# A GPS graph layer on one core: the last two node tiles go through one block per expert, the first returned rows go into places of sent tokens, the input flag is spread over the edge loop, chunks get smaller

## The chip, the core and the metric

The kernel runs on one core of one Trainium2 chip. The core has five engines with an instruction stream each: TensorE (PE, matrix products and transposes), VectorE (DVE), ScalarE (ACT), GpSimd (POOL) and SyncE (SP, which here only issues transfers). They share the on-chip memories SBUF (128 partitions) and PSUM (where matmuls write, in banks) and are kept in step by semaphores. Transfers to and from DRAM run on 16 DMA engines. A transfer is issued by an instruction on some engine's queue; an indirect one (rows picked by an index list) is issued by POOL here.

The metric is the device time of one execution, in microseconds (us). The kernel before takes 1828.77 us, the median of 8 runs between 1819.89 and 1846.31.

## The reference

All data are fp32. There are 6250 nodes with 256 features, and 106,250 edges, sorted by their destination, with 64 attributes each. The layer adds a message-passing branch and a linear-attention branch to the nodes, and then a feed-forward step in which each node uses one of 32 experts:

```python
xn = _layernorm(x)
# message passing: gather, project, silu, sum by destination, normalize
msgs = jnp.concatenate([xn[src], edge_attr], axis=-1)
msgs = jax.nn.silu(msgs @ W + b)
gnn  = _layernorm(jax.ops.segment_sum(msgs, dst, 6250), eps=1e-3) * gamma + beta
# linear attention, 8 heads of 64, k and v normalized over a head
dots = einsum('bhnd,bhne->bhde', k, v)
mix  = einsum('bhnd,bhde->bhne', q, dots) / n  @ Wout.T + bout
x = x + gnn + mix
# feed-forward with one expert per node
xf  = _layernorm(x)
idx = argmax(xf @ router_w.T + router_b)          # of 32
h   = relu(xf @ W1[idx] + b1[idx])                # 256 -> 64
out = x + relu(h @ W2[idx] + b2[idx])             # 64 -> 256
```

Since the projection is linear, the node part of `msgs @ W` is computed once per node and gathered afterwards.

## The kernel before

**Tiles.** The nodes are 49 tiles of 128 rows (the last has 106). `X` holds all of them in SBUF, `wide` holds their normalized, transposed rows and, once these are no longer needed, expert weights and tokens. The edges are 208 groups of 512; two groups make a step of the sum by destination.

**First stage** (`stage_one`, L254 to L484). Per pair of tiles: load, layernorm, transpose (L353), project (L363), add the bias (L369), store `proj` to DRAM. `columns` (L372) turns the source indices (at pair 3) and the destinations' offsets (at pair 10) into the layout of the loop, the latter after POOL has made them (at pair 6). At the end, `row_of` is made and then a flag: whether the destinations fit the windows that the loop assumes. This is a chain on DVE (L460 to L480), a matmul with ones (L482, `pflag`) and a copy into `unlike`. The flag is read only at the very end of the program, where a general path would follow if it were set. The pool `early` and the PSUM pool `pre_ps` are closed when `stage_one` returns; the loop's PSUM pool and the attention's SBUF pool open afterwards.

**Edge loop** (L1562 to L1603). For each group: four indirect gathers of `proj` rows on POOL, three groups ahead (L1432); the edge attributes turned (L1448, copied by ACT, L1452); their product `h` (L1571); DVE adds the gathered rows (L1573); ACT applies silu (L1589). Every second group, `level1` (L1526) and `level2` (L1553) sum the messages by destination. A tile whose edges are all in is closed, and a chunk of tiles (`CHUNKS`) is finished when its last tile is closed.

**The planner** (`Work`, L1287). All other work stands beside the loop as pieces: Python generators that write some instructions and then yield an estimated cost for PE and DVE, and a delay in turns. In each of the loop's turns `step` lets pieces advance until an allowance (2.7 us of PE, 3.8 us of DVE) is spent. In the last `QUIET = 4` turns only urgent pieces advance. After the loop `drain` (L1349) writes out what is left by a model of when the engines are free. So the order of instructions on every engine is fixed when the program is built. The pieces are: the attention's weights and batches, node chunks, rounds, clears of the blocks (L688), loads of the experts' weights.

**Chunks** (`Nodes.chunk`, L731). Finished tiles get the sum's layernorm (`sums_end`), the attention's product (`mixing`, L720), a second layernorm, the router's logits in groups of two tiles (transposes L784, `lg` L772), the argmax as a row of 0 and 1 (`hot`, L820), each token's rank within its expert (`prank`, L839 and L842; `ahead`, L846), and its place in a block (`slot`, L965). Then `send` (L1051) scatters each tile's rows into `xs` in DRAM.

**Rounds** (`Nodes.round`, L1265; `ROUNDS`). A round holds the tokens of some tiles as blocks of 64. The first round takes tiles 0 to 27 with 76 blocks, each with an expert chosen at run time; the next four (tiles 28 to 33, 33 to 38, 38 to 42, 42 to 47) have one block per expert. Four blocks make a quad (`tokens`, `layers`): load `xb` (L1066, on SP's queue), transpose (`pt`, L1088), first layer (`phid`, L1100; relu by ACT, L1110), second layer (`py`, biases L1124 and product L1135), relu (L1144), store to `ys` (L1146). When all quads of a round are done, `collect` (L1232) fetches the rows back by tile with indirect gathers (`fetch`, L1225), DVE adds them to `X` (L1248), and SP stores two tiles to the output (L160). In the drain the fetches' destinations are a ring of 4 `ot` pairs and 3 pairs of `wide`.

**The last round** is `(2, 0)`: tiles 47 and 48 are not sent. `dense` (L875 to L948) runs all 32 experts, two at a time, over their 234 rows: turned rows (L891) and turned `hot` rows (L895), bias of the second layer (L906), and for each of 16 pairs the first layer (L922), a masking product that pushes all rows of other experts below zero (L931), relu (L940), and the second layer (L914), summed over all experts in PSUM. Then relu, add and store.

**PSUM tags.** `kv` (two buffers) is shared by the attention's products, `lg`, `prank`, `phid` and, in the loop, both `py`; `t` (two buffers) by all transposes and `po`; `sum` and `h` by the loop's sums and products, and in the drain by `py`.

Of the kernel before, what the change touches and what calls it, by code (L numbers as in the profile page):

```python
# [31 lines left out]
CHUNKS = (6, 6, 6, 5, 5, 5, 5, 4, 3, 2, 2)  # L32
CH = max(CHUNKS)
FIRST = (2, 4, 6, 10, 13, 14)
AB = 2
# [6 lines left out]
BESIDE = 2  # L42
AHEAD_US = 1.0
# [4 lines left out]

ROUNDS = ((28, 76), (5, None), (5, None), (4, None), (5, None), (2, 0))
QUIET = 4  # L50
FAR = 3e38
# [11 lines left out]
def kernel(  # L63
# [190 lines left out]
    def stage_one(early, pre_ps):  # L254
# [133 lines left out]
        for j in range(NP + 1):  # L388
# [4 lines left out]
            if j == 3:  # L393
                nc.gpsimd.tensor_copy(src_f, src_r)
                columns(lambda b: src_f[:, b, :], src_T)
            if j == 6:
                nc.gpsimd.tensor_copy(dst_f, dst_r)
                nc.gpsimd.tensor_sub(rel, dst_f, dst_f[:, :, 0:1].to_broadcast([P, EB, P]))
            if j == 10:
                columns(lambda b: rel[:, b, :], rel_T)  # L400
# [56 lines left out]

# [5 lines left out]
        low, high = bounds(g_f, [P, EB], "tb")  # L463
        bad = early.tile([P, EB], F32, name="bad")
        nc.vector.tensor_reduce(bad, rel, axis=AX.X, op=ALU.max)
        nc.vector.tensor_scalar(bad, bad, float(SPAN), None, op0=ALU.is_ge)
        for source, op, limit, test in (
# [3 lines left out]
        ):  # L471
            some = early.tile([P, EB], F32, name="some", bufs=2)
# [8 lines left out]
        pb = bank("o", [1, 1], "pflag", 3)  # L481
# [134 lines left out]
    class Nodes:  # L616


        def __init__(self, pool, rounds, in_order):
# [36 lines left out]
            self.ring, self.returns = 7 if in_order else 4, 0  # L656
            self.started = self.through = self.flying = self.held = 0
            self.idle = pool.tile([1, 1], F32, name="idle")
            self.dense_in = False
# [43 lines left out]
        def sums_end(self, t0, t1):  # L703
# [3 lines left out]
            yield 0.0, 1.9, 1  # L707
            for t in range(t0, t1):
# [4 lines left out]
                if t % 3 == 2 or t == t1 - 1:  # L713
                    yield 0.0, 1.3, 1
# [16 lines left out]
        def chunk(self, t0, t1):  # L731
# [11 lines left out]
            for t in range(t0, t1):  # L743
# [6 lines left out]
                yield pe, dve + 0.6, int(t == t1 - 1)  # L750
            self.at[t0] = 1
            while not behind(2):
                yield 0.0, 0.0, 1
# [7 lines left out]
            yield 0.0, 1.9, 1  # L761
            logit = self.pool.tile([P, CH, NE], F32, name="logit", bufs=2)
            pairs = [list(range(t, min(t + 2, t1))) for t in range(t0, t1, 2)]
            turned = {}
            for i in range(len(pairs) + 2):
                pe = dve = 0.0
                if i >= 2:
                    lg = self.bank("kv", [P, 2, NE], "lg")
# [10 lines left out]
                    pe, dve = pe + 0.5, dve + 0.3  # L779
                if 1 <= i <= len(pairs):  # L780
                    for t in pairs[i - 1]:
# [3 lines left out]
                        turned[t] = self.pool.tile([P, DC, P], F32, name="xfT", bufs=2)  # L785
                        nc.scalar.copy(turned[t], pt)
                    pe += 0.5
# [36 lines left out]
            if r.dense:  # L824
                yield 0.0, 1.9, 1
                self.work.add(self.dense(t0, t1), rank=2)
                while not behind(4):
                    yield 0.0, 0.0, 1
                nc.vector.tensor_add(flag, self.over, unlike)
                return  # L830
# [26 lines left out]
            if r.own:  # L857
# [6 lines left out]
                if t1 == r.t1:  # L864
                    most = small.tile([1, 1], F32, name="most")
                    nc.vector.tensor_reduce(most, self.so_far[0:1, 0, :], axis=AX.X, op=ALU.max)
                    self.count(most, HB)
                self.at[t0] = 4
# [5 lines left out]

        def dense(self, t0, t1):  # L875


            m, pool = t1 - t0, self.last
            n = (m - 1) * P + rows_of(t1 - 1)
            of = [slice(k * P, min((k + 1) * P, n)) for k in range(m)]  # L880
            w = [q.stop - q.start for q in of]
            ident_b = pool.tile([P, P], BF16, name="ident_b")
            nc.vector.tensor_copy(ident_b, ident)
            far = pool.tile([NE, NE], BF16, name="far")
            nc.vector.tensor_scalar_mul(far, ident[:NE, :NE], -FAR)
            xT = pool.tile([P, DC, n], F32, name="xT")
            for k in range(m):
                pt = self.bank("t", [P, DC, P], "pt")
                feats = wide[:, t0 + k, :].rearrange("p (q c) -> p c q", c=DC)
                for c in range(DC):  # L890
                    nc.tensor.transpose(pt[:, c, :], feats[:, c, :], ident)  # L891
                nc.scalar.copy(xT[:, :, of[k]], pt[:, :, : w[k]])
            ph = self.bank("kv", [NE, n], "phot")
            for k in range(m):
                nc.tensor.matmul(  # L895
                    ph[:, of[k]], self.hot[:, t0 + k, :], ident_b[:, : w[k]], start=True, stop=True
                )
            hotT = pool.tile([NE, n], F32, name="hotT")
            nc.vector.tensor_copy(hotT, ph)
            other = pool.tile([NE, n], BF16, name="other")  # L900
            nc.vector.tensor_scalar(other, ph, -1.0, 1.0, op0=ALU.mult, op1=ALU.add)
            yield 1.0, 0.6, 1
            self.dense_in = True
            py = [self.bank("sum", [P, D], f"py{k}") for k in range(m)]
            for k in range(m):
                nc.tensor.matmul(py[k][: w[k], :], hotT[:, of[k]], self.b2_sb[:NE, :], start=True, stop=False)  # L906
            yield 0.9, 0.0, 0
            hids, pairs = {}, NE // BB
            for q in range(pairs + 2):
                if q >= 2:  # L910
                    hid = hids.pop(q - 2)
                    w2_q = wide[:, (q - 2) // 2 * QB + BB + q % 2, :]
                    for k in range(m):
                        nc.tensor.matmul(  # L914
                            py[k][: w[k], :], hid[:, of[k]], w2_q, start=False, stop=(q - 2 == pairs - 1)
                        )
# [905 lines left out]
```

## Time and profile before

| | us |
|---|---|
| median of 8 runs | 1828.77 (1819.89 to 1846.31) |
| the profiled execution | 1844.18, of it 1842.5 in the span |
| first stage, to the last projection's end | 79 |
| edge loop, to the last sum (L1553) | about 99 to 1699.3 |
| from there to the end | 143.2 |

| engine | busy us | share of the span | instructions |
|---|---|---|---|
| PE | 1281.7 | 70% | 8301 |
| DVE | 825.4 | 45% | 2107 |
| ACT | 567.2 | 31% | 1046 |
| POOL | 940.6 | 51% | 1046 |

The DMA engines moved 227.6 MB, 124 GB/s on average. Mean granted clock of PE: 0.81 of full speed. The profile is of one execution, which is 15.4 us above the median of the plain runs.

How to read the lines further on. A group line gives the source line, the engine, the operation, output and inputs by the program's names, shapes and count; after the bar its busy time in us and the mean of one in ns; after the second bar the engine's idle time just before those instructions and what ended most of it ("issue" means nothing that the profile shows). A line of waits gives engine and line, what it waited for, the total in us, how often, and the longest. A timeline line gives start, duration, engine, line, operation, and in brackets the idle time before it with what ended it. A line of windows is explained where it is used.

### The profile page before, as it was taken

Reading aid. Unit: us, or ns where it says so; the run is one execution under the profiler, and the core shown is the slowest. Engines: PE = TensorE matmul, PEld = TensorE weight load, DVE = VectorE, ACT = ScalarE, POOL = GpSimd, SP = SyncE. Lnnn points to the kernel's source line nnn. Section 1 sums busy time; section 2 is a strip of 40 time slices with the busy share of each in tenths; the row PEclk is TensorE's granted clock in tenths of the full one; section 3 lists DMA queues with packets and bytes.
Section 4 is the critical chain, followed back from the end, with each engine's and each line's share of the span. In section 5 each row is a group of like instructions: output and inputs, shape, how many; then the busy total and the mean of one; then the engine's idle time right before and its main releaser. Section 6 shows DMA issues by size and latency. Waiting matters only on the chain. (4 is left out here: it accounts for less than half of the span.)

```text
span 1842.5 us, 24393 instructions
## 1 busy us (share of the span) xinstructions
PE 1281.7 (70%) x8301; PEld 740.5 (40%) x8301; DVE 825.4 (45%) x2107; ACT 567.2 (31%) x1046; POOL 940.6 (51%) x1046
## 2 busy tenths in 40 slices
PE   6747888788858888677766652655776667676557
PEld 5624444444434444444434421333443334343324
DVE  7734555555545565465554532332333133434420
ACT  4524444344334344222322211222222123232213
POOL 4535665666646566655654666453343434441541
PEclk9968989998979989877877766776777678877669
DMA  6383333343323334633432343455454444342443
GB/s 218 128 268 97 111 110 102 104 111 105 106 80 106 89 106 120 207 90 85 109 97 78 105 145 118 136 159 148 128 149 125 121 134 131 115 118 68 123 161 128
DMA packets 243794, 227.60 MB, mean 124 GB/s; under 512 B 130920, under 2 KB 213836, under 8 KB 243660
## 3 DMA queue, kind: packets, MB, share of 16 engines
q0 software_dynamic: 44384, 121.18, 22.3%
q1 hardware_dynamic: 91096, 77.41, 13.1%
q10 hardware_dynamic: 108180, 27.34, 6.5%
q8 instruction: 69, 1.13, 0.3%
q14 instruction: 65, 0.53, 0.1%
HBM read 180.14 MB, written 45.70 MB: 123 GB/s over the span
## 5 line engine op out<-in xcount | busy, mean ns | idle before, releaser
L1432 POOL DMA_INDIRECT gat<-proj,src_T x831 | 800.8, 964 | 744.1 <-issue 598.3
L1573 DVE TENSOR_TENSOR gat<-h,gat 128x1024 f32<-128x1024 f32 x208 | 254.2, 1222 | 452.8 <-PE h L1571 134.1
L1571 PE MATMUL h<-ge,eT 64*128 64x256 f32 x1664 | 284.2, 449 | 140.6 <-DVE gat L1573 59.5
L1571 PEld LDWEIGHTS h<-ge,eT 64*128 64x128 f32 x1664 | 170.2, 210 | 252.2 <-issue 154.7
L1589 ACT ACTIVATE gat<-gat 128x1024 f32<-128x1024 f32 x208 | 219.9, 1057 | 167.9 <-DVE gat L1573 116.2
L1553 PE MATMUL sum<-part,s 128*128 128x256 f32 x400 | 138.1, 475 | 94.8 <-DVE s L1542 71.8
L540 PE MATMUL kv<-kv_w,wide 128*128 128x512 f32 x392 | 197.9, 650 | 3.2 <-DVE kv_w L518 3.2
L1452 ACT COPY eT<-pt 128x256 f32<-128x256 f32 x208 | 77.5, 373 | 348.2 <-remote 179.1
L1526 PE MATMUL po<-gat,s 128*32 128x256 f32 x1664 | 147.7, 453 | 11.7 <-issue 10.7
L1535 ACT COPY part<-po 128x256 f32<-128x256 f32 x104 | 38.7, 372 | 377.0 <-PE po L1526 181.4
L1553 PEld LDWEIGHTS sum<-part,s 128*128 128x128 f32 x400 | 86.0, 234 | 133.1 <-DVE s L1542 79.5
L540 PEld LDWEIGHTS kv<-kv_w,wide 128*128 128x128 f32 x392 | 79.5, 215 | 85.6 <-issue 80.5
L1448 PE MATMUL pt<-ident,ea 128*128 128x128 f32 x416 | 99.7, 325 | 9.8 <-DVE dots L575 4.1
L1094 DVE COPY xbT<-pt 128x512 f32<-128x512 f32 x39 | 26.9, 689 | 160.7 <-remote 76.1
L1526 PEld LDWEIGHTS po<-gat,s 128*32 128x32 f32 x1664 | 52.4, 124 | 91.5 <-issue 75.6
L1448 PEld LDWEIGHTS pt<-ident,ea 128*128 128x128 f32 x416 | 45.0, 152 | 89.8 <-issue 68.1
L547 DVE TENSOR_REDUCE var<-sq 128x16 f32<-128x1024 f32 x49 | 59.7, 1218 | 46.0 <-ACT sq L546 26.7
L1124 PE MATMUL py<-b_sb,choseno 32*64 32x256 f32 x152 | 29.5, 491 | 66.2 <-ACT hid L1110 19.8
L720 PE MATMUL pres<-mix,wide 128*128 128x256 f32 x196 | 60.5, 446 | 20.5 <-DVE experto L1030 8.8
L1051 POOL DMA_INDIRECT xso<-wide,slot x47 | 47.2, 1005 | 51.4 <-DVE slot L965 27.1
L543 ACT COPY kv<-kv 128x512 f32<-128x512 f32 x98 | 54.5, 578 | 34.5 <-PE kv L540 19.0
L1124 PE MATMUL py<-b_sb,ident 32*64 32x256 f32 x256 | 36.2, 465 | 41.5 <-ACT hid L1110 19.4
(298 smaller groups left out, 1533.1 us busy)
## 6 DMA issues: line engine op xcount, KB each, us to landing
ea<-in_edge_attr_dram ACTq DMA_DIRECT2D x203, 128.0 KB
gat<-proj,src_T POOLq DMA_INDIRECT x831
xso<-zero SPq DMA_DIRECT2D x51, 256.0 KB
xb<-xso SPq DMA_DIRECT2D x51, 256.0 KB
yso<-xb SPq DMA_DIRECT2D x51, 256.0 KB
proj<-pr SPq DMA_DIRECT2D x24, 256.0 KB
out_dram<-X SPq DMA_DIRECT2D x22, 256.0 KB
w1t<-in_L_ffn_W_dram SPq DMA_DIRECT2D x76, 64.0 KB
```

What stands on the lines that cost most here:

```text
L540: nc.tensor.matmul(b, xnT(t0 + j, c), kv_w[:, c, s * F : (s + 1) * F], start=(c == 0), stop=(c == DC - 1))
L547: nc.vector.tensor_reduce(var[:, j * 2 * HEADS : (j + 1) * 2 * HEADS], sq, axis=AX.X, op=ALU.add)
L720: nc.tensor.matmul(p, xnT(t, c), mix[:, c, :], start=(c == 0), stop=(c == DC - 1))
L1124: nc.tensor.matmul(py[j][i * HB : (i + 1) * HB, :], one_of(b, rows).to_broadcast([NE, HB]), self.b2_sb[rows, :], start=True, stop=False, t ...
L1432: nc.gpsimd.indirect_dma_start(out=gat[:n, k % 2, k // 2, :], out_offset=None, in_=proj[:], in_offset=bass.IndirectOffsetOnAxis(ap=src_T[: ...
L1448: nc.tensor.transpose(pt[:, j, :], ea[:, 2 * j : 2 * j + 2, :].rearrange("p k d -> p (k d)"), ident)
L1452: nc.scalar.copy(eT, pt)
L1526: nc.tensor.matmul(po[k * wide_k : (k + 1) * wide_k, :], s1[:, k, :], msg[:, k % 2, k // 2, :], start=(g == here[0]), stop=(g == here[-1]) ...
L1553: nc.tensor.matmul(sums[t], s2[:, (t - lo) * P : (t - lo + 1) * P], part, start=(q == opens[t]), stop=(q == closes[t]),)
L1571: nc.tensor.matmul(h[:, s, j, :], eTs[g][half, j, :], ge[half, :], start=True, stop=True)
L1573: nc.vector.tensor_add(gats[g], h, gats[g])
L1589: nc.scalar.activation(gats[g], gats[g], AF.Silu)
```

## The change

Six things are edited together.

1. `ROUNDS` ends in `(2, None)`: tiles 47 and 48 are a round like the four before it, with one block per expert, that is 8 quads, two sends, two fetches. `dense` and all that mentions it is removed. The flag is then completed by the last chunk.
2. `CHUNKS` cuts the first 28 tiles into six chunks in place of five, of at most 5 tiles; the router takes its tiles in up to groups of `TG = 3`.
3. In `stage_one`, the index columns are made some pairs later, and the flag's chain becomes steps of a generator that `attention` runs in the loop before it loads its weights; `pflag` uses the loop's bank `kv`, and `early` closes after that.
4. `phid` uses the bank `t` in the loop, and `kv` in the drain.
5. `collect` takes five pairs of `wide` (tiles 32 to 41, whose tokens are sent by then) before it takes `ot` pairs, and may use them before the drain.
6. The planner: in the quiet turns, chunk pieces and pieces for POOL go on and POOL's queue is issued at once; in the drain chunk pieces are urgent, each other piece is held back by its own engine alone, and two quads may be between their start and their first layer; a round waits for its own sends rather than for all of POOL's planned work; steps at a chunk's start get an earlier due time (`AT_ONCE`), and a chunk's stages wait for 1.5 and 2 of the chunk before.

```diff
-CHUNKS = (6, 6, 6, 5, 5, 5, 5, 4, 3, 2, 2)
+CHUNKS = (5, 5, 5, 5, 5, 3, 5, 5, 4, 3, 2, 2)
+TG = 3
+AT_ONCE = -9.0
-ROUNDS = ((28, 76), (5, None), (5, None), (4, None), (5, None), (2, 0))
+ROUNDS = ((28, 76), (5, None), (5, None), (4, None), (5, None), (2, None))
...
     def stage_one(early, pre_ps, later_bank):
...
         nc.vector.scalar_tensor_tensor(row_of, row_of, r_f, starts, op0=ALU.add, op1=ALU.subtract)
+        yield
         g_i = early.tile([P, EB], I32, name="g_i")
...
         low, high = bounds(g_f, [P, EB], "tb")
+        yield
         bad = early.tile([P, EB], F32, name="bad")
...
+            if limit is high:
+                yield
...
         nc.vector.tensor_reduce(bad1, bad, axis=AX.X, op=ALU.add)
-        pb = bank("o", [1, 1], "pflag", 3)
+        yield
+        pb = later_bank("kv", [1, 1], "pflag")
...
             self.at[t0] = 1
-            while not behind(2):
+            while not behind(1.5):
                 yield 0.0, 0.0, 1
...
-            if r.dense:
-                yield 0.0, 1.9, 1
-                self.work.add(self.dense(t0, t1), rank=2)
...
-        def dense(self, t0, t1):
...
         def layers(self, pool, r, b0, xb, w1_of, w2_of, b1_of, one_of):
-            while self.through < self.started:
+            while self.started - self.through > int(self.work.draining):
                 yield 0.0, 0.0, 1
...
-            ph = self.bank("kv", [P, QB // BB, HB], "phid")
+            ph = self.bank("kv" if late else "t", [P, QB // BB, HB], "phid")
...
-            elif b0 // QB % 2 and not self.dense_in:
+            elif b0 // QB % 2:
...
         def collect(self, r, t0, t1):
-            while self.held + t1 - t0 > 2 * self.ring:
+            while not self.beside and (not self.last or self.held == 4):
                 yield 0.0, 0.0, 1
-            self.held += t1 - t0
-            at = self.returns % self.ring - 4
-            self.returns += 1
-            if at < 0:
+            at = self.beside.pop(0) if self.beside else None
+            if at is None:
+                self.held += 1
                 both = self.last.tile([P, 2, D], F32, name="ot", bufs=4)
...
             yield 0.0, 0.0, 2, self.work.pool_free - self.work.now + 7.0
+            while not self.work.draining:
+                yield 0.0, 0.0, 1
...
         def on_pool(self, issue):
-            if self.work.draining:
+            if self.work.draining or self.work.quiet:
                 self.work.issue(issue)
...
         def round(self, pool, r):
-            yield 0.0, 0.0, 2, self.work.pool_free - self.work.now + 2.5
+            yield 0.0, 0.0, 2, r.sent_by - self.work.now + 2.5
...
         def step(self, allowance, quiet=False):
-            if quiet:
-                return
+            self.quiet = quiet
+            while quiet and self.pool:
+                self.issue(self.pool.pop(0))
...
-                while piece.due <= self.turn and min(self.left) > 0 and not piece.done:
+                while not (quiet and piece.rank and piece.by != "pool") and piece.due <= self.turn and min(self.left) > 0 and not piece.done:
                     self.advance(piece)
...
         def drain(self):
+            self.pool_free = 0.0
             for piece in self.pieces + self.urgent:
                 piece.due = self.now
+                piece.urgent |= not piece.rank
...
-                    busy = (self.pool_free if piece.on_pool else max(self.free)) - self.now
-                    if piece.due <= self.now and (piece.urgent or busy <= AHEAD_US):
+                    loads = {"pe": self.free[0], "dve": self.free[1], "pool": self.pool_free, None: max(self.free)}
+                    if piece.due <= self.now and (piece.urgent or loads[piece.by] - self.now <= AHEAD_US):
...
             def attention():
+                for _ in first_stage:
+                    yield 0.0, 3.8, 0
+                early_scope.close()
+                attn = attn_scope.enter_context(tc.tile_pool(name="attn", bufs=1))
```

## The prediction

> **What bounds the kernel now.** I read the busy tenths of the page first. TensorE (PE) is the busiest engine, 1281.7 of 1842.5 us, but its row is not full anywhere after the first stage, so no engine's total sets the time. I then cut the span into windows. Two places have a long idle PE: the join between the first stage and the edge loop (80 to 120 us), and everything after the last sum of the loop at 1699.3 us, which I call the tail. Both are among what the diff edits. Columns: busy us and instructions of PE, its weight loads, DVE, ACT, POOL; then granted clock, DMA share, GB/s.
>
> ```profile
> 60.00:80.00 20.00, 19.64 (x109) 16.81 (x107) 8.48 (x19) 12.12 (x25) 10.93 (x17) 1.00 0.39 136
> 80.00:100.00 20.00, 1.93 (x12) 1.34 (x14) 16.25 (x63) 0.81 (x3) 11.62 (x12) 0.61 0.45 122
> 100.00:120.00 20.00, 4.41 (x20) 2.45 (x17) 2.04 (x4) 2.71 (x3) 11.50 (x12) 0.50 0.80 275
> ...
> 1720.00:1730.00 10.00, 0.17 (x1) 0.18 (x2) 1.24 (x4) 1.37 (x4) 4.84 (x6) 0.50 0.27 80
> 1760.00:1770.00 10.00, 2.66 (x10) 0.64 (x6) 2.77 (x4) 0.00 (x0) 7.62 (x8) 0.50 0.49 155
> 1770.00:1780.00 10.00, 2.29 (x4) 0.70 (x4) 2.77 (x4) 0.00 (x0) 6.67 (x7) 0.50 0.36 105
> 1790.00:1800.00 10.00, 10.00 (x108) 6.05 (x106) 0.00 (x0) 4.72 (x13) 0.00 (x0) 1.00 0.40 133
> ```
>
> PE does 6.3 us in 40 us of the join; in the tail it does 0.17, 2.66 and 2.29 us in windows of ten, and is full from 1790 to 1830. So the tail is first a chain with stalls and then pure matmul. The groups say which matmuls (the first two lines are the join, the others the tail, from 1699 us on), and the whole run's waits name a third place, the psum bank of `phid`:
>
> ```profile
> L482 PE MATMUL pflag<-ones,bad 128*1 128x1 f32 x2 | 0.2, 164 | 17.9 <-DVE bad L480 17.9
> L1571 PE MATMUL h<-ge,eT 64*128 64x256 f32 x16 | 4.2, 671 | 15.8 <-ACT eT L1452 15.6 <-issue 0.2
> ...
> L914 PE MATMUL py<-wide,hid 128*128 128x256 f32 (+1 forms) x64 | 17.3, 395 | 0.0
> L922 PE MATMUL pre<-xT,wide 128*64 128x234 f32 x128 | 17.0, 388 | 4.6 <-issue 4.6
> L1135 PE MATMUL py<-wide,hid 64*64 64x256 f32 x104 | 16.7, 448 | 0.0
> L931 PE MATMUL pre<-other,far 32*64 32x234 bf16 x32 | 5.0, 286 | 2.9 <-issue 2.9
> ...
> PE phid L1100 <- ACT xb L1144: 28.3, 10, 7.7
> ```
>
> Last, the timeline, for who is late for whom (start, duration, idle time before):
>
> ```profile
> 97.39 0.16 DVE L480 TENSOR_REDUCE bad<-bad 128x1 f32<-128x7 f32 x1
> 111.51 1.23 DVE L1573 TENSOR_TENSOR gat<-h,gat 128x1024 f32<-128x1024 f32 x1 [12.23 <-DMA gat<-proj,src_T]
> 1707.22 1.23 POOL L1051 DMA_INDIRECT xso<-wide,slot  x1 [27.11 <-DVE slot L965]
> 1738.11 1.26 POOL L1051 DMA_INDIRECT xso<-wide,slot  x1 [0.21 <-issue]
> 1822.92 0.95 POOL L1225 DMA_INDIRECT ot<-yso,back  x1 [44.19 <-DMA yso<-xb]
> ```
>
> PE sat from 79.7 to 97.6 us for a flag that nothing in the loop uses; POOL's last fetches wait for the last quad's store while 30 fetches ran between 1739.68 and 1778.7, just where PE crept.
>
> **Part 1, dense pairs against quads.** From the chain of waits, one dense pair costs 0.87 (L914) + 0.94 (L922) + 0.21 (L931) = 2.02 us of PE, 16 pairs 32.3; its preparation 0.9 (L891) + 0.3 (L895) + 1.2 (L906) = 2.4. Removed: 34.7 us. Added: 8 quads of 0.68 (L1088) + 0.61 (L1100) + 0.43 (L1124) + 1.01 (L1135) = 2.73, that is 21.8. Difference -12.9 on a PE that is full there. The 8 added loads and 8 stores (256 KB each) and the clears go through SP, covered by PE's own work: the last full windows run at a DMA share of 0.40 to 0.54. Uncovered they would cost 16 issues of 0.37 us, 6 us.
>
> **Part 2, the end gets longer.** Today dense finishes in SBUF: last L914 at 1831.9, end 1842.5, 10.6 us. A quad's rows must come back: in the existing last quad L1135 ends at 1819.3 and the first fetch starts at 1822.9, 3.6; two fetches at 1.26 apart, 2.2; landing 2.2 and two adds 0.9 (from the rows of L1248 after the last fetches); stores to the end 9.3. That is 18.2, so +7.6.
>
> **Part 3, the chain and the stalls.** Before, router and places of tiles 45 to 47 run 1709.4 to 1735.9, with a hole to 1728.7 that ends as POOL's 15 back-to-back indirect DMAs (1707.2 to 1726.3) end. Sends are out at 1738.1, and the next quads' rows have landed at 1748.5, 9.1 after. The same chain for tiles 47 to 49 (their `hot` is made at 1737.7) now goes on to places: 8.3 us without a hole, 18.8 as for the pair before. With two sends (2.5) and 9.1, its rows are in at 1758 to 1768. PE does the 8 quads of tiles 42 to 47 from 1748.5 to 1770 and the last 8 to 1792; plus 18.2 is 1810, 32 us earlier than 1842.5. That needs the creep of 1754 to 1783 gone, which cost 29 less about 5 of work, 24: with it the end is 1834, -8. The order of the new instructions puts, behind the sends of tiles 42 to 45, 10 fetches while the loop still runs and 16 after it; behind the sends of 45 to 47 stand 6, and then the sends of 47 to 49. So a stream of 6 stands where 30 stood, and I count the creep half gone: **-20** for parts 1 to 3, between -32 and -8. Two fetches share one tile pair each, and a reused pair waits for DVE's add, 0.69 us, beside.
>
> Why a stream of POOL should hold PE the profile doesn't say. One rule speaks against it. The Trainium skill, "SBUF — State Buffer", section "Who interferes with whom", says that DMA never contends with a compute engine; by it the creep is no effect of the fetches and would stay where it is, and the tail would give -8 alone. The timeline shows single L1124 matmuls 2.1 to 2.8 us apart for as long as POOL streams, so I hold the row for the likelier.
>
> **Part 4, the flag.** 9.6 us of DVE work (87.89 to 97.55) leave the join for five steps in the loop, where DVE is 45% busy; price 0, or +9.6 if it finds no gap. The matmul L482 goes with it. PE can then do the first group's h from 80 on, but its first DVE add at 111.51 waited for more than the flag: POOL's 24 gathers run 84.9 to 115.0, and the clears fill the DMAs from 101 on. Bounds: 0 (those hold it as they do now) and -20 (111.5 less 91.3, when the first gathers had signalled). I take one turn of the loop, **-8** (1600 us by 208 groups is 7.7), because only group 0 fits ahead of 99. Attention's weights come some four turns later; the order of instructions leaves the same 5 quads of tiles 38 to 42 to the tail, so nothing else slides.
>
> **Part 5, the bank.** `phid` leaves "kv", where it waited 28.3 us for L1144 to empty `py`. Ends: 0 (the next wait, on "t" with `po` and `pt`, is as long) and -28. I take **-5**: PE mostly has other work queued beside and the loop's pace is one group's chain.
>
> **Part 6, sizes.** One more chunk in the first 28 tiles is two more inverse-root chains, some 22 DVE instructions of 0.2, 4.4 us; groups of three router tiles save small ones. Hidden under DVE's 55% idle: 0, up to +4.4.
>
> **Sum.** -20 - 8 - 5 = -33 on the profiled execution's 1844.18: 1811. That execution is 15.4 us over the median; by 1828.77/1844.18 = 0.9916 the forecast is **1796 us**. All lower ends, -32 - 20 - 28 = -80, give 1749; all upper, -8 + 9.6 + 4.4 = +6, give 1835.
>
> **The rivals.**
> (a) Faster, but the creep stays: -8 and the flag's -8, 1828 profiled, 1813 as median. For it: the DMA engines were full just as the creep began (share 1.04, 359 GB/s from 1750 to 1760), and quads' loads, stores and fetches will crowd there again. Against: the creep ends with the stream.
> (b) No change: the flag's time is behind the gathers (0), the bank's behind the group chain (0), and part 2 with slower places eats part 1; 1822 to 1838. For it: at 111.51 DVE waited for a gather, not for the flag. Against: 54 of 143 us of the tail are idle PE.
> (c) Slower. The 26 fetches from before the loop's end on are one stream of 26 x 1.26 = 33 us. If streams hold PE, a stream of that length cost 32.5 us before (24.6 + 7.9 us of gaps in the 32 of 1736.8 to 1778.7), and the hole of 11 us now in the router's chain becomes 32: +21, before the sends and so in front of all 16 last quads; the later fetches keep the creep. -12.9 + 7.6 + 21 = +16, less nothing at the start: 1860 profiled, 1844 median. It decides once the added hole is over 5.3 + 13 (what the other parts gave), 18 us. For it: the hole of 1717 to 1728 lies on that chain. Against: 10 of the 26 lie beside the loop's last groups, and in the loop's streams of 16 PE's longest gap between two signals was 6 to 8.
>
> **How the numbers follow.** Forecast 0.47, (a) 0.25, (b) 0.10, (c) 0.18. A change of 0.5% is about what a measurement of this kernel can tell, 9 us: faster 0.72, same 0.10, slower 0.18. The range runs from 1764 (-32 for the tail, -20 for the start and -13, half of the bank's bound, are -65 and give 1779 x 0.9916) to 1832, which holds (a) and most of (b) and leaves out (c).
>
> **What would show it.** L482 with no idle ahead and the first L1573 before 105 us: part 4. The last quad's L1135 at 1785 to 1800 and the end 18 us behind: parts 1 and 2. No window of ten under 3 us of PE after the sends of tiles 45 to 47: part 3. The wait of L1100 on L1144 under 10 us: part 5. A hole of over 20 us in the router's chain right after the loop would be (c), and the forecast would be wrong; so too if the loop's own last sum came later than 1699.

## The result, and the profile after

The changed kernel is slower: 1.0106 of the kernel before, 95% interval 1.0084 to 1.0128 (median 1851.41 us of 23 runs against 1830.86 of 65), and 1.0059 [1.0027, 1.0091] when it was measured again (run `a_same`). The forecast was 1796 us, faster. One thing about the numbers that follow: in two of the five sets of runs the kernel before took 1365 and 1362 us and not 1835, 1856 and 1850 (one chip gave both kinds), so a ratio is always taken within its own set.

I cut both profiled executions at the starts of DVE's adds of gathered rows, one per group (L1573 before, L1525 after). This is what each stretch took, in us:

| stretch | before | after | difference |
|---|---|---|---|
| start to add of group 2 | 129.5 | 121.6 | -7.9 |
| group 2 to 24 | 141.7 | 143.4 | +1.7 |
| group 24 to 48 | 150.8 | 169.5 | **+18.7** |
| group 48 to 112 | 430.9 | 427.8 | -3.1 |
| group 112 to 144 | 235.2 | 269.4 | +34.2 |
| group 144 to 200 | 554.9 | 516.2 | -38.7 |
| group 200 to 207 | 49.7 | 58.4 | **+8.7** |
| last add to the end | 149.8 | 143.2 | -6.6 |
| span | 1842.5 | 1849.5 | +7.0 |

The profiled execution of before lies 13 us above its median and that of after at its own, so the table holds only 7 of the 20 us between the medians; it tells where to look, the runs decide. The +34.2 and -38.7 nearly cancel, and I did not find out why. It is not the first round moved forward: up to group 144 neither kernel has started a quad, and PE's busy time in that stretch differs by only 3.5 us (155.1 and 151.6). What stays is a loss between groups 24 and 48, a loss in the last eight groups, and a gain in the tail far below the forecast. The loop's last sum came at 1714.9 us, later than the 1699 that the prediction had named as a sign of being wrong.

The windows of the changed kernel, at the join and in the tail (columns as in the prediction):

```profile
80.00:100.00 20.00, 6.96 (x32) 3.96 (x30) 9.44 (x37) 4.42 (x7) 10.89 (x11) 0.59 0.46 125
100.00:120.00 20.00, 2.70 (x10) 1.56 (x10) 8.93 (x31) 1.43 (x2) 12.47 (x14) 0.50 0.34 98
...
1745.00:1755.00 10.00, 2.78 (x18) 2.21 (x18) 7.74 (x30) 0.74 (x2) 6.48 (x9) 0.71 0.87 275
1755.00:1765.00 10.00, 4.49 (x37) 3.61 (x38) 6.03 (x21) 1.17 (x2) 7.73 (x11) 0.50 0.73 234
1785.00:1795.00 10.00, 10.00 (x130) 6.60 (x126) 0.00 (x0) 5.93 (x18) 0.00 (x0) 0.91 0.48 159
1825.00:1835.00 10.00, 0.46 (x6) 0.00 (x0) 1.03 (x2) 0.77 (x2) 1.71 (x2) 0.63 0.35 110
1835.00:1850.00 15.00, 0.00 (x0) 0.00 (x0) 0.85 (x2) 0.00 (x0) 0.80 (x1) 0.50 0.11 31
```

The join has 9.7 us of PE in 40 where it had 6.3, so it is still nearly empty. In the tail PE is still thin around the sends and nearly full from 1785 to its last product at 1825.5, where the forecast had the last quad at 1785 to 1800; then come 24 us in which PE does nothing at all. The creep of single matmuls is there too, shorter than in before: from 1766 to 1781 us PE does 24 matmuls, beside ten fetches that POOL issues behind the last sends, the last of them at 1778.4:

```profile
1774.36 1.30 PE L1069 MATMUL py<-wide,hid 64*64 64x256 f32 x2 [0.73 <-issue]
1776.49 0.68 PE L1069 MATMUL py<-wide,hid 64*64 64x256 f32 x1 [0.83 <-issue]
...
1778.38 0.95 POOL L1159 DMA_INDIRECT wide<-yso,back  x1 [0.30 <-issue]
```

Why the join stays empty stands in the timeline of the changed kernel, POOL's rows and then DVE's:

```profile
105.05 0.95 POOL L1381 DMA_INDIRECT gat<-proj,src_T  x1 [0.30 <-issue]
106.00 0.16 POOL L462 IOTA g_i<- 128x7 int32 x1
106.33 0.96 POOL L1381 DMA_INDIRECT gat<-proj,src_T  x1 [0.17 <-issue]
...
92.89 1.23 DVE L1525 TENSOR_TENSOR gat<-h,gat 128x1024 f32<-128x1024 f32 x1 [4.00 <-DMA gat<-proj,src_T]
106.20 0.17 DVE L463 TENSOR_SCALAR g_i<-g_i 128x7 int32<-128x7 int32 x1 [11.89 <-POOL g_i L462]
113.68 1.23 DVE L1525 TENSOR_TENSOR gat<-h,gat 128x1024 f32<-128x1024 f32 x1
```

The first add comes at 92.9 us and not at 111.5, as hoped. But the flag's chain begins with an `iota` on POOL. In the first stage that stood ahead of all gathers; behind the first `yield` it stands in POOL's queue after 16 of them. DVE works in order, so it waits 11.89 us for it with the next group's add queued behind.

The end, where two sends, loads, quads, stores and fetches now follow each other (the last quad's product, relu, store; the two fetches; the two adds):

```profile
1824.38 1.08 PE L1069 MATMUL py<-wide,hid 64*64 64x256 f32 x8
1825.07 0.81 ACT L1078 ACTIVATE xb<-py 128x256 f32<-128x256 f32 x2 [0.51 <-PE py L1069]
1825.93 1.31 SPq L160 DMA_DIRECT2D out_dram<-X  x2
1827.34 0.95 SPq L1080 DMA_DIRECT2D yso<-xb  x2
1832.98 0.94 POOL L1159 DMA_INDIRECT wide<-yso,back  x1 [12.83 <-DMA yso<-xb]
1834.23 1.57 POOL L1159 DMA_INDIRECT wide<-yso,back  x1 [0.31 <-issue]
1835.88 0.43 DVE L1190 TENSOR_TENSOR X<-wide,X 128x256 f32<-128x256 f32 x1 [9.64 <-DMA wide<-yso,back]
1840.18 0.42 DVE L1190 TENSOR_TENSOR X<-wide,X 106x256 f32<-106x256 f32 x1 [3.88 <-DMA wide<-yso,back]
```

The last store of `ys` waits on SP behind two output stores of tiles that came back earlier, its rows take until 1832.9 to land, and the second fetch needs 6 us more until DVE can add it. From PE's last product to the end pass 24.0 us (1849.5 less 1825.5).

### The profile page after: what moved, and what is told of

Same layout as the page of the kernel before. It is cut to its first block, busy times and chain, and to the rows that moved or that the text cites. A ratio compares the mean times of both kernels' runs of the same rounds, so it can differ in the third digit from the quotient of the medians.

```text
span 1849.5 us, 24668 instructions
## 1 busy us (share of the span) xinstructions
PE 1254.9 (68%) x8363; PEld 730.8 (40%) x8363; DVE 830.3 (45%) x2147; ACT 574.3 (31%) x1066; POOL 940.7 (51%) x1052
## 3 DMA queue, kind: packets, MB, share of 16 engines
q0 software_dynamic: 44960, 121.67, 22.5%
## 5 line engine op out<-in xcount | busy, mean ns | idle before, releaser
L1525 DVE TENSOR_TENSOR gat<-h,gat 128x1024 f32<-128x1024 f32 x208 | 254.1, 1222 | 458.4 <-remote 195.8
L1523 PE MATMUL h<-ge,eT 64*128 64x256 f32 x1664 | 280.2, 445 | 153.5 <-DVE gat L1525 91.6
L1505 PE MATMUL sum<-part,s 128*128 128x256 f32 x400 | 143.5, 491 | 138.8 <-DVE s L1494 115.9
L547 PE MATMUL kv<-kv_w,wide 128*128 128x512 f32 x392 | 193.0, 636 | 3.5 <-issue 2.4
L1505 PEld LDWEIGHTS sum<-part,s 128*128 128x128 f32 x400 | 88.8, 241 | 178.0 <-DVE s L1494 123.2
L1487 ACT COPY part<-po 128x256 f32<-128x256 f32 x104 | 38.7, 372 | 357.4 <-PE po L1478 172.5
L1159 POOL DMA_INDIRECT wide<-yso,back x41 | 40.6, 990 | 75.1 <-DMA yso<-xb 47.7
L1078 ACT ACTIVATE xb<-py 128x256 f32<-128x256 f32 x118 | 42.9, 381 | 94.5 <-PE py L1069 37.4
L1069 PE MATMUL py<-wide,hid 64*64 64x256 f32 x320 | 59.0, 485 | 16.6 <-ACT hid L1044 14.0
```

The costliest lines, as they stand in the source:

```text
L547: nc.tensor.matmul(b, xnT(t0 + j, c), kv_w[:, c, s * F : (s + 1) * F], start=(c == 0), stop=(c == DC - 1))
L1069: nc.tensor.matmul(py[j][i * HB : (i + 1) * HB, :], hid[half, j, :], w2_of(BB * j + i, half), start=False, stop=True, tile_position=(i * H ...
L1505: nc.tensor.matmul(sums[t], s2[:, (t - lo) * P : (t - lo + 1) * P], part, start=(q == opens[t]), stop=(q == closes[t]),)
L1523: nc.tensor.matmul(h[:, s, j, :], eTs[g][half, j, :], ge[half, :], start=True, stop=True)
L1525: nc.vector.tensor_add(gats[g], h, gats[g])
```

## The experiments

**Each part alone on the kernel before.** The theories: the forecast's prices part by part, against one place each where a part could lose.

`b_phid`: only the bank of `phid`.

```diff
-            ph = self.bank("kv", [P, QB // BB, HB], "phid")
+            ph = self.bank("kv" if late else "t", [P, QB // BB, HB], "phid")
```

> Before, with only the bank of phid changed (tag t in the loop). Theory A (the bank made the edge loop slower: with phid in t the loop's own transposes queue behind the quad's xbT copy): ratio 1.005 to 1.012, a wait of pt L1448 on DVE xbT of about 45 us that before doesn't have, and the wait of phid on ACT xb (28 us) gone. Theory B (the bank is harmless, as forecast, and the loss is in the quiet turns and the tail): ratio 0.993 to 1.000.

Measured 0.9962 [0.9923, 1.0]. The forecast's side. Its waits show both theories' mechanism: the wait on "kv" is gone from the list, and one on "t" has come, longer than the old one:

```profile
PE pt L1448 <- DVE xbT L1094: 49.2, 7, 8.2
```

A sum of one kind of wait is thus no price: these 49 us took the place of others. The interval reaches 1.0, so alone the gain is not clear of nothing; two pairs further on, each within one set, point the same way (`b_flag_iota` and `b_two`, `b_flag0_iota` and `b_best`).

`b_flag`: only the spread flag and the later index columns (part 3 of the change).

> Before, with only the flag's chain spread into the loop and the index columns made later. Forecast: first add of gathered rows near 93 us rather than 111.5, and the whole 8 us shorter, ratio 0.996. Theory B': the 8 us are lost again in the first 40 groups, since attention's weights come later: ratio 1.000 or above.

Measured 1.0084 [1.005, 1.0118]. The first add is at 92.8 us as in the changed kernel, the lead is 8.2 us at group 2, 5.5 at group 24, and at group 40 it is a lag of 14.5. Alone this part costs nearly as much as the whole change, and theory B' names the right place. It is not the only one: `b_last`, next, costs as much again.

`b_last`: only the last two tiles as a round.

```diff
-ROUNDS = ((28, 76), (5, None), (5, None), (4, None), (5, None), (2, 0))
+ROUNDS = ((28, 76), (5, None), (5, None), (4, None), (5, None), (2, None))
...
+                    if t1 == NT:
+                        nc.vector.tensor_add(flag, self.over, unlike)
```

> Before, with only the last two tiles as a round with one block per expert (dense left out, the flag completed by the last chunk). Forecast, parts 1 and 2: -12.9 + 7.6, so ratio 0.993 to 0.999. Theory C (the chain of send, load, quads, store, fetch at the end is longer than dense, which needed no transfer): ratio 1.004 to 1.012, last matmul earlier than in before, but the end more than 18 us behind it.

Measured 1.0096 [1.0058, 1.0133]. Theory C. The last matmul is at 1823.8, 8.5 us earlier than in before, but the loop ended that much earlier in this execution; measured from the loop's last sum it comes no earlier (133.4 us behind it, 133.1 in before). The end is 24.9 us behind it rather than 10.1; from the last add of gathered rows to the end it is 165.1 us and not 149.8. The other parts of the change take some of that back: in the changed kernel this stretch is 143.2. Two windows of `b_last` show PE in this stretch:

```profile
1750.00:1760.00 10.00, 1.97 (x8) 0.76 (x8) 3.25 (x6) 0.52 (x2) 7.56 (x9) 0.50 0.46 133
1760.00:1770.00 10.00, 1.12 (x16) 0.94 (x16) 2.60 (x5) 0.59 (x1) 7.56 (x9) 0.50 0.36 103
```

From 1737 to 1777 us PE does 10.9 us of work in 40, beside 26 fetches that POOL issues from 1740 to 1773; in before the creep was 29 us (1754 to 1783) with 7.1 of work.

`b_chunks`: only `CHUNKS`, the router in groups of two as before.

```diff
-CHUNKS = (6, 6, 6, 5, 5, 5, 5, 4, 3, 2, 2)
+CHUNKS = (5, 5, 5, 5, 5, 3, 5, 5, 4, 3, 2, 2)
```

> Before, with only the first 28 tiles in six chunks rather than five (the router still in groups of two). Forecast: nothing, ratio 0.998 to 1.002. Theory D (each chunk's chain of small DVE instructions is on the loop's path in the middle third): ratio 1.003 or more.

Measured 1.0024 [0.9961, 1.0087]: undecided. The four parts add up to +1.66%, the change is +1.06% or +0.59%; the planner's part and the fetches into `wide`, which I did not run alone, would then have gained about 0.6 to 1.1%. That is a difference of intervals and not a measurement.

**What in the flag loses.** In this set before took 1364.77 us.

`b_delay`: the flag stays, the attention starts three turns later.

```diff
             def attention():
+                for _ in range(3):
+                    yield 0.0, 3.8, 0
                 w = {}
```

> Before, the flag left where it is; the attention only starts three turns later, which charge the planner what the flag's steps charge it. b_flag alone took 1.0084 [1.005, 1.0118]. Theory E (the loss of b_flag is the later start: attention, clears and expert weights move against the groups, and POOL's gathers run together into streams of 16): ratio 1.008 to 1.014, since the 8 us gained at the start are not there to set against it, and the adds of groups 24 to 40 fall behind as in b_flag. Theory F (the flag's own DVE work in the loop costs it): ratio 0.998 to 1.003.

Measured 0.999 [0.9975, 1.0006].

`b_flag0`: the spread flag in one turn, at no charge to the planner.

```diff
                 for _ in first_stage:
-                    yield 0.0, 3.8, 0
+                    pass
```

> b_flag with its steps in one turn and at no charge to the planner: the flag's DVE chain stands in the first turn of the loop, the attention starts as early as in before. Theory E: ratio 0.994 to 0.999, groups 24 to 40 as in before. Theory F: ratio 1.005 or more, as b_flag.

Measured 1.0076 [1.0055, 1.0097]. Here theory E fell and F seemed to hold, and the timeline of `b_flag0` gave F its mechanism, the one seen above in the changed kernel:

```profile
104.80 0.17 DVE L463 TENSOR_SCALAR g_i<-g_i 128x7 int32<-128x7 int32 x1 [11.89 <-POOL g_i L462]
...
114.64 0.19 PE L489 MATMUL pflag<-ones,bad 128*1 128x1 f32 x2 [25.81 <-DVE bad L486]
```

PE, which waited 17.9 us for the flag in the first stage, now waits 25.8 us for it in the loop.

`a_unflag`: the changed kernel with the flag back in the first stage.

```diff
+                stage_one(early, pre_ps)
...
-                for _ in first_stage:
-                    yield 0.0, 3.8, 0
-                early_scope.close()
```

> The changed kernel with the flag and the index columns put back into the first stage, all else as changed (ratio of the changed kernel: 1.0106). Theory G (the parts add up, and the flag is the loss): 1.0106 - 0.0084, ratio 1.000 to 1.004. Theory H (the loss is in the last round and the planner, the flag being one of several ways to the same stall): ratio 1.008 or more.

Measured 1.0065 [1.0042, 1.0088], between G and H. In its profile the last add of gathered rows comes at 1251.0 us, as in `b_delay` (1250.8), which took as long as before; all that is lost is in the tail, 117.2 us against 109.2. Its chain of waits (start, duration) shows how:

```profile
1332.60 3.00 DMA xb<-xso
1335.60 0.14 issue
...
1344.48 1.03 PE py L1062 x8
1345.54 0.39 ACT xb L1071
1345.93 1.37 SPq L1073
1347.40 2.68 DMA yso<-xb
1350.29 0.70 issue
1350.98 0.88 POOL wide L1152
1352.00 0.24 issue
1352.24 6.53 DMA wide<-yso,back
1358.87 0.42 DVE X L1183
```

PE ends 4.4 us earlier than in `b_delay` (1345.5 and 1349.9) and not the 12.9 that its work is less: at 1332.6 it waits for a quad's rows. Then 22.7 us follow, against 10.0.

`b_nofetch`: the 47 fetches after the loop left out, with a memset for each pair.

```diff
-            for t in range(t0, t1):
-                self.on_pool(lambda t=t: self.fetch(r, both[:, t - t0, :], t))
+            self.on_pool(lambda: nc.gpsimd.memset(both[:, : t1 - t0, :], 0.0))
```

> Before, with the 47 indirect fetches after the loop left out (a memset stands in for each pair, so tiles 0 to 46 lack the experts' part). Theory S (streams of indirect transfers on POOL hold PE's signals up): no window of ten under 5 us of PE between 1750 and 1780, the end 20 to 35 us earlier, ratio 0.981 to 0.990. Theory T (the creep is of the loads and stores or of PE itself): creep stays, ratio 0.994 to 1.001.

Measured 0.9988 [0.9972, 1.0003]: theory T, or nothing to see, since here the creep is absent with the fetches as well. That itself tells against my reading of the streams. The tail of `b_delay`, an unchanged tail with all its fetches:

```profile
1300.00:1310.00 10.00, 10.00 (x105) 6.27 (x106) 3.19 (x5) 4.87 (x14) 7.56 (x9) 1.00 0.98 333
1310.00:1320.00 10.00, 10.00 (x104) 6.20 (x104) 2.34 (x4) 4.77 (x14) 7.56 (x9) 1.00 0.99 336
```

POOL streams fetches without a pause, the DMA engines are full, and PE is at 10.00 of 10. A stream on POOL is not enough to make PE creep. For the other level this run says nothing: there the creep ended within 5 us of the stream in before, in `b_last` and in the changed kernel, and no run left the fetches out. The rule that the prediction weighed (the Trainium skill, "SBUF — State Buffer", section "Who interferes with whom", that DMA never contends with a compute engine) agrees with these rows, and I had set it aside.

**The head of the flag's chain.** In this set before took 1856.02 us.

`a_same` is the changed kernel; `a_iota` and `b_flag_iota` are the changed kernel and `b_flag` with one instruction moved; `b_two` is `b_flag_iota` with `phid` in "t".

```diff
-        yield
         g_i = early.tile([P, EB], I32, name="g_i")
         nc.gpsimd.iota(g_i, pattern=[[P, EB]], base=0, channel_multiplier=1)
+        yield
```

> The changed kernel itself, beside the three that follow. On the chip where before takes 1831 us its ratio was 1.0106. On the other chip, where before takes 1365 us, theory I (the flag's chain waits behind POOL's gathers, +0.0076 there, and the tail, +0.0065 there) gives 1.012 to 1.016; theory H (the parts are several ways to one stall and don't add) 1.005 to 1.009.

> The changed kernel with one instruction moved: POOL's iota g_i, the head of the flag's chain, is written before the loop's first gathers rather than behind 16 of them. Theory I: DVE's chain starts right after the first add instead of at 106 us, the adds of groups 2 to 24 come 8 to 15 us earlier than in the changed kernel, ratio to before lower by 0.005 to 0.011 than the changed kernel's. Theory J (POOL's queue is not the cause, the loop's later loss of groups 24 to 40 is): no change beyond 0.002.

> Before with the spread flag, and the iota written before the first gathers. Theory I: ratio 0.994 to 0.999 (the forecast's 8 us). Theory J: 1.005 to 1.010, as b_flag (1.0084) and b_flag0 (1.0076).

> Before with the two parts that should gain: the spread flag with its iota first, and phid in bank t (alone 0.9962). If the parts add, ratio 0.990 to 0.996, faster than both kernels; if phid's gain is only a shift of the loop's stalls, 0.996 to 1.002.

Measured 1.0059 [1.0027, 1.0091], 1.0047 [1.0019, 1.0075], 1.006 [1.003, 1.009] and 1.0031 [1.0003, 1.0059]. By the times theory J holds: the moved `iota` takes 0.0012 from the changed kernel's ratio, and `b_flag_iota` stays slow; `b_two` lies outside both of its ranges. By the trace theory I's wait was there: the add of group 2 comes at 108.7 and 106.5 us in the kernels with the moved `iota`, not at 121. But `b_flag_iota` is 13.4 us ahead of before at group 24 and 13.0 behind at group 48. A second cause eats the gain between the two.

**The second cause.** `b_delay2` and `b_delay3` are `b_delay` once more; `b_flag0_iota` is `b_flag0` with the `iota` moved as above, `b_best` and `b_best2` are that with `phid` in "t" as well, and `a_flag0` is the changed kernel with the edits of `b_flag0` and of `a_iota`. First set, where before took 1361.8 us:

> b_delay once more (the flag stays in the first stage, the attention starts three turns later), wanted on a chip where before takes 1830 to 1856 us; on the other it took 0.999. Theory E (the later start of the attention is what the spread flag loses by: its pieces catch up between groups 24 and 48, by 20 us in all five kernels with the spread flag): a loss of 10 to 20 us between groups 24 and 48 against before, ratio 1.005 to 1.012. Theory J2 (the loss there needs the flag's own instructions): ratio 0.997 to 1.002.

> Before, the flag's chain in the loop's first turn, at no charge to the planner, with its iota ahead of the gathers: neither POOL's queue nor a later attention. Theory E: the lead of 10 to 20 us at group 24 stays to the end of the loop, ratio 0.989 to 0.996 (on a chip where before takes 1365 us, 0.995 to 1.001, since its join has less idle time). Theory J2: the lead is lost by group 48, ratio 1.002 or more.

> b_flag0_iota with phid in bank t. If both gains hold and add: 0.985 to 0.993. If phid's gain is not stable (it was 0.9962 [0.9923, 1.0] alone): as b_flag0_iota within 0.003.

> The changed kernel with the same mending: iota ahead of the gathers, the flag's steps in one turn at no charge. Changed kernel: 1.0106 and 1.0059 in its two measurements. Theory E: 0.993 to 1.000. If the tail and the later loop hold all of the loss: 1.004 or more.

Measured 0.9989 [0.9972, 1.0006], 1.0015 [0.9998, 1.0032], 0.9901 [0.9875, 0.9926] and 1.0101 [1.0071, 1.0131]. The moved `iota` takes `b_flag0` from 1.0076 (in the set with `b_delay`) to 1.0015, between the two expectations. `b_best` beats the kernel before. The changed kernel stays slow with the flag mended, at this level; at the other `a_flag0` was not run, nor the changed kernel itself at this one. Its tail is 116.2 us against 109.4 in `b_delay2`, and it lacks the gain of the bank (its loop ends at 1256.4, that of `b_best` at 1235.0), so the remaining parts cost it in the loop too. Which of them, I did not separate.

Then the two kernels that tell the theories apart, in a set where before took 1850.42 us:

> b_best again (flag's chain in the first turn with its iota first, phid in bank t), wanted on a chip where before takes 1830 to 1856 us; on the other it took 0.9901. Theory E there: no loss of 20 us between groups 24 and 48, the lead of group 24 is kept, ratio 0.982 to 0.992. Theory J2: 20 us lost between groups 24 and 48, ratio 0.997 to 1.004, as b_two (1.0031).

> b_delay again (attention three turns later, the flag in the first stage), for the same reason; on the other chip 0.999 and 0.9989. Theory E on a chip of 1830 to 1856 us: 10 to 20 us lost against before between groups 24 and 48, ratio 1.005 to 1.012. Theory J2: none lost, 0.997 to 1.002.

Measured 0.9961 [0.9925, 0.9997] and 1.0126 [1.0074, 1.0178]. For the stretch in question that is theory E, though both times lie just outside its ranges. `b_best2` loses nothing between groups 24 and 48, but its lead at group 24 is 2.1 us and not 10 to 20: with the whole chain in one turn DVE works it off before the second add, and PE waits 13.4 us for it, so the add of group 2 comes at 128.7 us (106.7 in `b_two`, where the chain is spread). From the add of group 24 to that of group 48, all executions profiled at this level:

| attention starts | kernels | us |
|---|---|---|
| as in before | before, `b_phid`, `b_last`, `b_chunks`, `b_best2` | 150.8, 149.1, 149.5, 148.8, 151.0 |
| three turns later | after, `a_same`, `a_iota`, `b_flag`, `b_flag_iota`, `b_two`, `b_delay3` | 169.5, 179.3, 177.9, 171.7, 177.2, 169.8, 172.6 |

No kernel lies between the two rows, and `b_delay3` has the flag where before has it, while `b_best2` has it in the loop. The same stretch as windows, first `b_best2`, then `b_delay3`:

```profile
268.00:440.00 172.00, 145.29 (x885) 75.23 (x885) 94.02 (x216) 70.06 (x109) 107.51 (x111) 0.89 0.39 106
```

```profile
268.00:440.00 172.00, 128.51 (x810) 68.64 (x808) 84.34 (x192) 62.38 (x97) 94.13 (x98) 0.87 0.35 93
```

In equal time the late starter does 17 us less on PE and about a tenth less on every engine: it isn't busier, it stands still. One place where the order of its instructions differs: up to the add of group 28 the attention's `kv` products are level again (112 in `b_delay3`, 113 in before); then 8 come in four groups and 24 in the next four, where `b_best2` has 16 and 16, and before 20 and 19. But part of the loss comes ahead of that, since groups 24 to 28 take 35.6 us in `b_delay3` and 25.7 in before. The timeline of `b_flag` at this first bad turn, where PE stands still for 10.4 us:

```profile
283.45 1.13 PE L1583 MATMUL h<-ge,eT 64*128 64x256 f32 x8
284.51 0.44 PE L1457 MATMUL pt<-ident,ea 128*128 128x128 f32 x2
...
295.53 1.23 DVE L1585 TENSOR_TENSOR gat<-h,gat 128x1024 f32<-128x1024 f32 x1 [12.24 <-remote]
298.38 0.37 ACT L1461 COPY eT<-pt 128x256 f32<-128x256 f32 x1 [8.83 <-remote]
...
298.81 1.65 PE L1583 MATMUL h<-ge,eT 64*128 64x256 f32 x6 [10.42 <-ACT eT L1461]
```

By PE's rows its products were done at 284.6 and 285.0, and DVE and ACT took them up at 295.5 and 298.4, when PE's semaphore moved (295.5 and 298.3): PE's signal came late. The ends of PE's rows are modelled, so the rows don't tell whether the products themselves were late. That the late start costs some 20 us here is shown; that the catching up is how, or what holds the signal, is not. At the other level the same order of instructions (`b_delay`, `b_delay2`) took 122.8 and 121.4 us for these groups, `b_flag0_iota` without the late start 121.3, and lost nothing.

## Why the prediction was wrong, by its own steps

**Part 4, the flag, is the step that failed**, in the sentence "the order of instructions leaves the same 5 quads of tiles 38 to 42 to the tail, so nothing else slides". The 8 us at the start came (7.9 at group 2), but by a lucky sum: 18.6 at the first add, and 11.9 lost again to POOL's `iota`, an instruction that is moved past 16 transfers and that I never counted. I had listed the 9.6 us of DVE work and PE's matmul, and no other engine's share of the moved chain. And what slid was the attention: three turns later at the start, level again by group 28, and 20 us lost between groups 24 and 48. I compared the two orders at the end of the loop only. As measured, part 4 is not -8 but +0.84% [0.5, 1.18], about +15 us of 1835, on the kernel before. **The last round, parts 1 and 2 together, is the second step that failed:** forecast -12.9 + 7.6, it measured +0.96% alone (`b_last`), about +18 us.

**Part 2, mis-sized.** The end behind PE's last product is 24.0 us (24.9 in `b_last`), not 18.2. The row that I had taken the first term from, 3.6 us from a quad's product to its fetch, was of a store with a free SP queue; at the end it was 7.5: two output stores stood in front on SP, and the DMA share was 0.42 in these 7.5 us where it was 0.21 in the 3.6. Term by term the end took 7.5, 2.8, 4.4, 0.4 and 8.9 us (rows, two fetches, landing, adds, stores) where I had 3.6, 2.2, 2.2, 0.9 and 9.3.

**Part 1, right work, no effect alone.** PE has less to do as worked out, yet in `b_last` its last product is no earlier behind the last sum, not 12.9 us. The step that failed is that PE would be full there: `b_last` waits for no load, it creeps for 40 us instead of 29. In the changed kernel the last product is 110.6 us behind the last sum, 22.5 less than in before, with the planner's edits beside; what part 1 gave of that no run separates.

**Part 3.** The tail gained 8.7 us from the last sum of the loop on (134.5 against 143.2), close to the upper bound of my -32 to -8, not the middle. The creep itself was about half gone, as I had counted: 15 us for 29. Of the 11.3 us that are missing to the forecast's 123.2 (143.2 less 20), the longer end is 5.8; the rest is PE's last product, 110.6 us behind the last sum where the forecast had 105. The last send of tiles 45 to 47 started 39.4 us after the last sum, as before (38.8): the fetches put ahead bought nothing there. The last eight groups got 8.7 us longer; the largest part of it, a step of 9.9 us for 3.3 from group 205 to 206, lies beside the ten fetches put ahead (1690.6 to 1703.1 us), which is no proof that they are the cause.

**Part 5** was right in sign and near in size: -0.38% is 7 us, with 5 forecast, though the interval reaches 0 and the wait on "t" that I had named as a reason for 0 came, at 49 us. So the size was luck; where the gain comes from is not shown. **Part 6**, nothing, is not contradicted.

**The rivals.** (c) had the right side and nearly the right time, 1844, for a wrong reason: no hole of 32 us opened in the router's chain, and the sends left no later. Its condition, that streams on POOL hold PE, is refuted as a general law by the tail of `b_delay`; at the level of the forecast it stands untested. The failure is one of coverage: a moved generator was costed by its busy time, and neither the queue it was moved into nor the work it pushed back was followed.

## What to carry to other kernels

When a piece of work is moved, list every engine that issues a part of it, and read what stands ahead of each in the new queue: one `iota` of 0.16 us behind 16 gathers held DVE for 11.9 us. When a planner charges the moved work to its budget, compare the orders turn by turn, not at the end, and move it at no charge if the engine is idle anyway (`b_two` and `b_best2` differ in this alone: 1.0031 with the charge and 0.9961 without, each in its own set). It has a price: with all of it in one turn the add of group 2 came 22 us later (128.7 and 106.7). A last stage that returns through memory ends a store, a fetch, a landing and an output store after its last product; price each by a row from a loaded queue.

## What the runs showed of the hardware

The same program ran at two levels, 1362 to 1365 us and 1831 to 1856 us, on one chip even. The first page lines of `b_delay` (1359.9 us) and, in the second fence, of before (1842.5 us) show what differs (`b_delay` is before with the late start, and took 0.999 of it; before itself was not profiled at the lower level):

```profile
PE 1121.1 (82%) x8301; PEld 670.1 (49%) x8301; DVE 824.5 (61%) x2107; ACT 566.2 (42%) x1046; POOL 943.6 (69%) x1046
```

```profile
PE 1281.7 (70%) x8301; PEld 740.5 (40%) x8301; DVE 825.4 (45%) x2107; ACT 567.2 (31%) x1046; POOL 940.6 (51%) x1046
```

DVE, ACT and POOL take the same time to the percent; PE takes 14% more, at a mean granted clock of 0.81 against 0.92, and stands still for most of the rest. Gaps of over 6 us between two of PE's signals are 54 in before and 8 in `b_delay`. So the time goes with PE's pace, and the price of a change differs between the levels: the late start of the attention costs 1.3% at one and nothing at the other, POOL's late `iota` 0.6% at the lower one (with the chain in one turn) and 0.1 to 0.2% at the higher (with it spread, so not quite the same pair). What makes PE's signals late is open.
